# Attention's score maxima reach their contraction row by one transfer per head, and a query tile takes every fourth query

## The chip, the cores and the metric

The kernel runs on one core of one Trainium2 chip. The metric is device time in microseconds (us) of one execution; lower is better. Profiles come from one profiled execution of the same program. The engines are named as in the profile: PE is TensorE's matmul, PEld its weight load, DVE is VectorE, ACT is ScalarE, POOL is GpSimd, and SP is the queue that issues nearly all DMA transfers.

## The reference, cut to what matters

Eight sequences (`B = 8`) of 512 tokens with 512 features go through one decoder layer in float32: a Mamba block, cross attention with 16 heads of 32 features, and a mixture of 32 experts, each with its residual and a layer norm. The change touches attention's softmax alone:

```python
qm = _split_heads(q @ Wq.T + bq)
km = _split_heads(k @ Wk.T + bk)
vm = _split_heads(v @ Wv.T + bv)
scores = jnp.einsum('bnlh,bnph->bnlp', qm, km) / np.sqrt(HEAD_DIM)
scores = jnp.where(mask, scores, MASK_FILL)
attn = jax.nn.softmax(scores, axis=-1)
out = jnp.einsum('bnlp,bnph->bnlh', attn, vm)
```

## The kernel before

**Three parts.** `layers` holds Mamba, attention and the shared expert (in the profile from 0 to about 3790 us), `experts` the 32 routed experts (to about 5270 us), `finish` the last layer norm. The change lies in `layers`.

**Two streams of work in one loop.** The main loop goes over 16 chunks (8 sequences, 2 chunks of 256 tokens each) and in each over 32 steps of Mamba's scan. A step has three large DVE instructions: `steps_in` (L494), `scan` (L501) and `collect` (L510), some 4.7 us in all. For each step ACT makes the decays `l_da` (L480) from rows that a DMA has repeated over partitions (`rep`, L428), and PE sums products of the scan into `py` (`products`, L519 and L521). Products of a step read the tile `h` (six buffers), so a later `steps_in` waits for them. Beside it the loop works off a list of side work, `todo`: attention and the shared expert of the sequence before it. Each entry has a weight, and the loop takes entries so that weights spent keep pace with steps done. The last sequence has no scan beside it: its attention runs by itself, from about 3600 to 3710 us.

**Attention of one sequence** (`units`). Heads go in eight pairs. The tiles `qa` and `ka` of a pair hold for each of its two heads 64 rows: 32 rows of queries (or keys), and 32 more for terms that are added to the scores by the same matmul. One of those rows of `qa` is for the maximum of each query, and the row of `ka` against it holds a constant. For a pair:

- `spread(i)` fills `qa` and `ka` and clears the row of maxima.
- `maximum(i, lt)`, four times: PE makes the scores of 128 queries (stationary: a slice of `qa`) against 512 keys, for both heads (L813), and DVE takes the maximum over keys, of both heads at once (L815), into two columns of the tile `mx`.
- `negate(i)`: PE transposes `mx` into a PSUM tile `ps_m` (four transposes, L822), ACT multiplies by -1 into a tile `nm` (L826), and two DMAs write its two rows into the row of maxima of `qa` (L829).
- `weigh(i, kc)`, four times: PE makes the scores the other way round, keys by queries, now with the maximum subtracted by the contraction itself (L839), and ACT takes the exponential (L843).
- `gather(i, kc)`: PE multiplies by the values (L855), the sums of weights come along.

`maximum` runs six places ahead of `weigh`, and the list alternates: a `maximum`, a `weigh`, a `gather`. Entries are made by

```python
if late:
    add(0.4, negate, late.pop(), dry=True)
if m < pairs * SC:
    add(0.9, maximum, m // SC, m % SC)
```

**What decides the order on an engine.** The functions emit instructions in the order of the loop, and a part that a function returns (a DVE or ACT instruction that reads what PE made) is emitted a little later. The framework then lays out each engine's instructions, and each engine works through its own in order. The score tiles `ps_s` and `ps_t` share two PSUM buffers (pool `l_pss`), so that a score matmul of `maximum` waits until the DVE maximum of the tile two before it is done. `ps_m` is one of the many users of the two buffers "mm" (pool `l_psm`), `nm` one of those of the two buffers "row" (pool `l_p3`).

Of the kernel before, what the change touches and what calls it, by code (L numbers as in the profile page):

```python
# [8 lines left out]
F32 = mybir.dt.float32  # L9
# [3 lines left out]
ALU = mybir.AluOpType  # L13
AX = mybir.AxisListType
# [3 lines left out]
P = 128  # L18
B, S, D = 8, 512, 512
DC = D // P  # L20
# [16 lines left out]
HD = 32  # L37
SC = S // P
# [50 lines left out]
def layers(ctx, tc, a, x1d, filld, based, xbuf):  # L89
# [23 lines left out]
    nc = tc.nc  # L113
# [3 lines left out]
    cp = ctx.enter_context(tc.tile_pool(name="l_const", bufs=1))  # L117
# [3 lines left out]
    p2 = ctx.enter_context(tc.tile_pool(name="l_p2", bufs=2))  # L121
    p3 = ctx.enter_context(tc.tile_pool(name="l_p3", bufs=2))
    dp = ctx.enter_context(tc.tile_pool(name="l_dram", bufs=2, space=DRAM))
    psm = ctx.enter_context(tc.tile_pool(name="l_psm", bufs=2, space=PSUM))
# [4 lines left out]
    ident = cp.tile([P, P], F32, name="l_ident")  # L129
# [7 lines left out]
    def rows(w):  # L137
        return w.rearrange("(c p) f -> p c f", p=P)
# [61 lines left out]

    ones = cp.tile([P, P], F32, name="l_ones")
    nc.gpsimd.memset(ones, 1.0)
    fold = cp.tile([P, QP], F32, name="l_fold")
    for at, sign in ((0, 1), (NQ - 1, -1)):
        nc.gpsimd.affine_select(
# [57 lines left out]
    def later_constants():  # L263

        nc.sync.dma_start(
            aneg.rearrange("p c j g -> p (c j) g"),
            a["A_log"].rearrange("(b c) (s g) -> (c s) b g", c=QP, s=NQ),
        )
        for i in range(NPB):
            for r0 in (HD + 1, 2 * HD + HD + 1):  # L270
                nc.sync.dma_start(
                    kas[i][r0 : r0 + 1, :].rearrange("p (c t) -> p c t", c=DC),
                    ones[0:1, :].unsqueeze(1).to_broadcast([1, DC, P]),
                )
        nc.sync.dma_start(bq, a["bq"])
        nc.sync.dma_start(bk, a["bk"])
        nc.sync.dma_start(bv, a["bv"].rearrange("(c p) -> p c", p=P))
        nc.sync.dma_start(bo, a["bo"].partition_broadcast(P))
        nc.sync.dma_start(wg, rows(a["wg"]))
# [473 lines left out]
    def units(b):  # L753

        st = {}
# [49 lines left out]
        def maximum(i, lt):  # L805

            qa, ka = st[i]
            if lt == 0:
                st["mx", i] = p2.tile([P, SC, 2], F32, tag="mx", name="mx")
            ps = pss.tile([P, 2, S], F32, tag="sc", name="ps_s")  # L810
            for j in range(2):
                r = slice(j * 2 * HD, (j + 1) * 2 * HD)
                nc.tensor.matmul(ps[:, j, :], qa[r, lt * P : (lt + 1) * P], ka[r, :], start=True, stop=True)  # L813
            mx = st["mx", i]
            return lambda: nc.vector.tensor_reduce(mx[:, lt, :].unsqueeze(2), ps, AX.X, ALU.max) and None  # L815

        def negate(i):

            mx = st.pop(("mx", i))
            pm = psm.tile([P, S], F32, tag="mm", name="ps_m")  # L820
            for lt in range(SC):
                nc.tensor.transpose(pm[0:2, lt * P : (lt + 1) * P], mx[:, lt, :], ident)  # L822

            def put():
                nm = p3.tile([P, D], F32, tag="row", name="nm")
                nc.scalar.mul(nm[0:2, :], pm[0:2, :], -1.0)  # L826
                for j in range(2):
                    r0 = j * 2 * HD + HD + 1
                    nc.sync.dma_start(st[i][0][r0 : r0 + 1, :], nm[j : j + 1, :])  # L829

            return put

        def weigh(i, kc):

# [128 lines left out]
        def add(weight, fn, *args, dry=False):  # L963

            todo.append((weight, lambda: fn(*args), dry))
# [14 lines left out]
        late = []  # L980

        def max_at(m):

            if late:
                add(0.4, negate, late.pop(), dry=True)
            if m < pairs * SC:
                add(0.9, maximum, m // SC, m % SC)
                if m % SC == SC - 1:
                    late.append(m // SC)

        for m in range(ahead):
            max_at(m)
        add(0, load, "sw1")
        for n in range(pairs * SC + 4):
            i, k = n // SC, n % SC
            if k == 0 and i + 2 < pairs:
                add(0, spread, i + 2)
            max_at(n + ahead)
            if i < pairs:
                add(0.9, weigh, i, k)  # L1000
            if 0 < n <= pairs * SC:
                add(0.9, gather, (n - 1) // SC, (n - 1) % SC)

            if n > 3 and (n - 3) % (2 * SC) == 0:
                add(0, divide, (n - 3) // (2 * SC) - 1, dry=(n > pairs * SC))
# [61 lines left out]
    def work(k):  # L1067

        front = 6.9 if k in (2, 3) else 3.4 if 4 <= k < 8 or k in (12, 14, 17, 20, 23) else 1.0 if k in (11, 25) else 0.0
        return 1.2 + front  # L1070
# [6 lines left out]
    for q in range(CC // 2):  # L1077
        do(convolve, 0, q, f, first=(q == 0))
    dry()
    later_constants()  # L1080
    silu(*f["xs"].values())
    do(x_proj, f)
# [16 lines left out]
    for i, (b, t) in enumerate(chunks):  # L1099
        nf = {}  # L1100
        after = chunks[i + 1] if i + 1 < len(chunks) else None
        if t == 0:
            side, spent = units(b - 1) if b else sources(0), 0.0

            own = [work(k) for k in range(len(steps))] * 2
# [411 lines left out]
def program(tc, a, out):  # L1517
    nc = tc.nc
    with tc.tile_pool(name="dram", bufs=1, space=DRAM) as dram:
        x1d = dram.tile([N, D], F32, name="x1d")  # L1520
        filld = dram.tile([B, S], F32, name="filld")

        based = dram.tile([N + P, D], F32, name="based")
        xbuf = dram.tile([SLOTS, ROW], F32, name="xbuf")
        nc.scalar.preload_act_table_set(LN_EXP)

        with ExitStack() as ctx:
            layers(ctx, tc, a, x1d, filld, based, xbuf)
        with ExitStack() as ctx:
            experts(ctx, tc, a, xbuf, based)  # L1530
        with ExitStack() as ctx:
            finish(ctx, tc, based, out)
# [31 lines left out]
```

## Time and profile before

| what | value |
| --- | --- |
| median of three runs | 5403.67 us (5400.97 to 5409.85) |
| profiled execution, its own time | 5406.28 us |
| span of its instructions | 5404.6 us |
| mean granted TensorE clock | 0.935 |
| PE, DVE, ACT, POOL busy over the span | 86%, 78%, 48%, 11% |
| 500 to 3520 us (scan with attention beside it): PE, DVE, ACT busy of 3020 us | 2545, 2748, 1779 us |
| 3600 to 3710 us (attention of the last sequence alone): PE, DVE, ACT busy of 110 us | 107, 45, 47 us |
| 3790 to 5270 us (experts): PE, DVE busy of 1480 us | 1473, 867 us |
| the transposes L822: count, busy | 256, 46.3 us |
| the ACT instructions L826: count, busy | 64, 37.2 us |
| the DMAs L829: count, time of one on SP's queue | 128, 553 ns (median) |

Busy time is the sum of an engine's instructions in a stretch. PE's times hold the time for which a matmul sits in the array behind another, so they overlap. An answer to "who waited for whom" names the instruction that waited, then what ended its wait, then the total, the number of times and the longest.

### The profile page before, as it was taken

Reading aid. Unit: us, or ns where it says so; the run is one execution under the profiler, and the core shown is the slowest. Engines: PE = TensorE matmul, PEld = TensorE weight load, DVE = VectorE, ACT = ScalarE, POOL = GpSimd, SP = SyncE. Lnnn points to the kernel's source line nnn. Section 1 sums busy time; section 2 is a strip of 40 time slices with the busy share of each in tenths; the row PEclk is TensorE's granted clock in tenths of the full one; section 3 lists DMA queues with packets and bytes.
Section 4 is the critical chain, followed back from the end, with each engine's and each line's share of the span. In section 5 each row is a group of like instructions: output and inputs, shape, how many; then the busy total and the mean of one; then the engine's idle time right before and its main releaser. Section 6 shows DMA issues by size and latency. Waiting matters only on the chain. (4 is left out here: it accounts for less than half of the span.)

```text
span 5404.6 us, 53991 instructions
## 1 busy us (share of the span) xinstructions
PE 4672.4 (86%) x17320; PEld 2476.6 (46%) x17320; DVE 4235.9 (78%) x5369; ACT 2593.6 (48%) x5726; POOL 570.3 (11%) x426
## 2 busy tenths in 40 slices
PE   6768889788888988988888888789999999999994
PEld 3324234234333423433333342333677777777773
DVE  7999899989989989898998998943566555665554
ACT  5566565565656556566565655523222222222223
POOL 1000002002000200200200020011111111111111
PEclk8879989999999999999999999899999999999997
DMA  8875346345444634634544463342344444544544
GB/s 236 266 224 146 87 96 208 81 114 176 114 104 117 197 77 109 189 98 107 174 125 100 117 200 78 91 146 66 103 128 127 123 117 118 127 127 121 129 115 144
DMA packets 486427, 719.03 MB, mean 133 GB/s; under 512 B 117137, under 2 KB 200625, under 8 KB 484096
## 3 DMA queue, kind: packets, MB, share of 16 engines
q1 hardware_dynamic: 450128, 627.16, 41.1%
q0 software_dynamic: 33280, 76.90, 7.5%
q10 hardware_dynamic: 2736, 11.54, 0.5%
q8 instruction: 137, 2.24, 0.2%
q14 instruction: 146, 1.20, 0.1%
HBM read 391.24 MB, written 165.05 MB: 103 GB/s over the span
## 5 line engine op out<-in xcount | busy, mean ns | idle before, releaser
L480 ACT ACTIVATE l_da<-rep,l_aneg 128x256 f32<-128x256 f32 x2048 | 895.0, 501 | 941.8 <-DVE h L501 877.0
L501 DVE TENSOR_TENSOR_SCAN h<-l_da,h 128x1028 f32<-128x1028 f32 x512 | 1166.0, 2292 | 20.3 <-ACT l_da L480 17.7
L494 DVE TENSOR_TENSOR h<-rep,bc 128x1024 f32<-128x1024 f32 x512 | 614.7, 1218 | 103.1 <-PE py L521 84.6
L510 DVE TENSOR_TENSOR h<-h,bc 128x1024 f32<-128x1024 f32 x512 | 619.5, 1217 | 2.1
L521 PE MATMUL py<-h,l_fold 128*32 128x512 f32 x2048 | 368.3, 644 | 113.4 <-DVE h L510 96.5
L813 PE MATMUL ps_s<-l_ka,l_qa 64*128 64x512 f32 x1024 | 325.6, 707 | 137.8 <-DVE mx L815 137.6
L1314 PE MATMUL ps_h<-xT,w 128*128 128x320 f32 x1536 | 435.8, 433 | 0.0
L1394 POOL DMA_INDIRECT based<-y,xe x160 | 255.5, 1597 | 1309.9 <-ACT y L1417 630.0
L1335 DVE TENSOR_TENSOR hT<-ps_h,p 128x320 f32<-128x320 f32 x128 | 62.9, 492 | 378.5 <-PE ps_h L1314 378.5
L815 DVE TENSOR_REDUCE mx<-ps_s 128x2 f32<-128x1024 f32 x256 | 310.2, 1217 | 58.5 <-PE ps_s L813 58.3
L1314 PEld LDWEIGHTS ps_h<-xT,w 128*128 128x128 f32 x1536 | 292.5, 191 | 118.3 <-issue 0.4
L855 PE MATMUL po<-eT,l_va 128*64 128x512 f32 x1024 | 301.5, 670 | 47.6 <-ACT eT L843 43.1
L839 PE MATMUL ps_t<-l_qa,l_ka 64*128 64x512 f32 x1024 | 308.4, 674 | 23.8 <-ACT eT L843 23.1
L843 ACT ACTIVATE eT<-ps_t 128x1024 f32<-128x1024 f32 x256 | 259.0, 1015 | 128.8 <-PE ps_t L839 128.5
L688 POOL DMA_INDIRECT xbuf<-x2t,dest x128 | 217.2, 1697 | 860.4 <-DVE dest L679 760.8
L1314 PE MATMUL ps_h<-t,s 128*128 128x320 f32 x1024 | 286.1, 432 | 0.0
L343 PE MATMUL ps_z<-xnT,wm 128*128 128x256 f32 x1024 | 238.0, 388 | 30.0 <-DVE o L561 24.3
L750 PE MATMUL ps_p<-x2T,wa 128*128 128x512 f32 x512 | 241.5, 626 | 18.1 <-ACT hT L944 10.4
L552 PE MATMUL po<-wm,zs 128*128 128x512 f32 x512 | 244.7, 632 | 13.8 <-DVE z L957 11.9
L343 PE MATMUL ps_x<-xnT,wm 128*128 128x256 f32 x1024 | 246.5, 393 | 4.5 <-ACT xnT L332 2.5
L343 PEld LDWEIGHTS ps_z<-xnT,wm 128*128 128x128 f32 x1024 | 194.6, 193 | 93.0 <-DVE o L561 37.5
L343 PEld LDWEIGHTS ps_x<-xnT,wm 128*128 128x128 f32 x1024 | 196.1, 195 | 80.5 <-issue 43.8
(232 smaller groups left out, 7170.4 us busy)
## 6 DMA issues: line engine op xcount, KB each, us to landing
w<-in_w SPq DMA_DIRECT2D x93, 1024.0 KB
wm<-in_in_proj_w SPq DMA_DIRECT2D x128, 512.0 KB
rep<-dt SPq DMA_DIRECT2D x256, 256.0 KB
rep<-dtx SPq DMA_DIRECT2D x256, 256.0 KB
xbuf<-zero SPq DMA_DIRECT2D x32, 1362.5 KB
xe<-xbuf SPq DMA_DIRECT2D x32, 1362.5 KB
wm<-in_out_proj_w SPq DMA_DIRECT2D x64, 512.0 KB
wa<-in_sw SPq DMA_DIRECT2D x24, 1024.0 KB
```

Of the source, the lines that this page charges most:

```text
L343: nc.tensor.matmul(ps[:, i, :], w[:, dc, i * P : (i + 1) * P], f["xnT"][:, dc, :], start=(dc == 0), stop=(dc == DC - 1),)
L480: nc.scalar.activation(da[:, n, 1:], dt[:, j, i, :], AF.Exp, scale=aneg[:, 2 * q + i, 2 * jj + j, g : g + 1])
L494: nc.vector.tensor_tensor(h[:, :, 1:], dtx.rearrange("p j i t -> p (j i) t"), f["bc", g][0], ALU.mult)
L501: nc.vector.tensor_tensor_scan(flat, da.rearrange("p n t -> p (n t)"), flat, 0.0, ALU.mult, ALU.add)
L510: nc.vector.tensor_tensor(h[:, :, 0:T], h[:, :, 1:], f["bc", g][1], ALU.mult)
L521: nc.tensor.matmul(f["py"][j * QP : (j + 1) * QP, :, :], fold, hs[j // 2][:, 2 * (j % 2) : 2 * (j % 2) + 2, 0:T], start=False, stop=g == N ...
L813: nc.tensor.matmul(ps[:, j, :], qa[r, lt * P : (lt + 1) * P], ka[r, :], start=True, stop=True)
L815: return lambda: nc.vector.tensor_reduce(mx[:, lt, :].unsqueeze(2), ps, AX.X, ALU.max) and None
L839: nc.tensor.matmul(ps[:, j, :], ka[r, kc * P : (kc + 1) * P], qa[r, :], start=True, stop=True)
L843: nc.scalar.activation(eT, ps, AF.Exp)
L855: nc.tensor.matmul(po[j * 2 * HD : (j + 1) * 2 * HD, :], va[:, kc, i, j * HD : (j + 2) * HD], eT[:, j, :], start=(kc == 0), stop=(kc == SC ...
L1314: nc.tensor.matmul(ps, w[:, n, r * P : (r + 1) * P], x[:, n, :], start=not more and n == 0, stop=n == 1, skip_group_check=more,)
```

## The change

The constant row of `ka` becomes -1 (it was 1), so that the row of `qa` takes the maxima as they are. Nothing has to be negated. A query tile `lt` no longer holds queries 128 lt to 128 lt + 127, but the queries lt, lt + 4, lt + 8 and so on: every fourth. Partition p of `mx` then holds the maxima of queries 4p to 4p + 3, and with its axes exchanged (`[P, 2, SC]`) these four lie side by side for each head. Read partition by partition, a head's 128 by 4 maxima are its 512 queries in order, and one DMA per head carries them from `mx` straight into the row of `qa`. The transposes, the PSUM tile, the ACT instruction and the tile `nm` are gone. The entry's weight goes from 0.4 to 0.

```diff
+    minus = cp.tile([1, P], F32, name="l_minus")
+    nc.gpsimd.memset(minus, -1.0)
...
                 nc.sync.dma_start(
                     kas[i][r0 : r0 + 1, :].rearrange("p (c t) -> p c t", c=DC),
-                    ones[0:1, :].unsqueeze(1).to_broadcast([1, DC, P]),
+                    minus.unsqueeze(1).to_broadcast([1, DC, P]),
                 )
...
             if lt == 0:
-                st["mx", i] = p2.tile([P, SC, 2], F32, tag="mx", name="mx")
+                st["mx", i] = p2.tile([P, 2, SC], F32, tag="mx", name="mx")
             ps = pss.tile([P, 2, S], F32, tag="sc", name="ps_s")
             for j in range(2):
                 r = slice(j * 2 * HD, (j + 1) * 2 * HD)
-                nc.tensor.matmul(ps[:, j, :], qa[r, lt * P : (lt + 1) * P], ka[r, :], start=True, stop=True)
+                own = qa[r, :].rearrange("k (p l) -> k l p", l=SC)[:, lt, :]
+                nc.tensor.matmul(ps[:, j, :], own, ka[r, :], start=True, stop=True)
             mx = st["mx", i]
-            return lambda: nc.vector.tensor_reduce(mx[:, lt, :].unsqueeze(2), ps, AX.X, ALU.max) and None
-
-        def negate(i):
+            return lambda: nc.vector.tensor_reduce(mx[:, :, lt].unsqueeze(2), ps, AX.X, ALU.max) and None
+
+        def subtract(i):
 
             mx = st.pop(("mx", i))
-            pm = psm.tile([P, S], F32, tag="mm", name="ps_m")
-            for lt in range(SC):
-                nc.tensor.transpose(pm[0:2, lt * P : (lt + 1) * P], mx[:, lt, :], ident)
-
-            def put():
-                nm = p3.tile([P, D], F32, tag="row", name="nm")
-                nc.scalar.mul(nm[0:2, :], pm[0:2, :], -1.0)
-                for j in range(2):
-                    r0 = j * 2 * HD + HD + 1
-                    nc.sync.dma_start(st[i][0][r0 : r0 + 1, :], nm[j : j + 1, :])
-
-            return put
+            for j in range(2):
+                r0 = j * 2 * HD + HD + 1
+                nc.sync.dma_start(st[i][0][r0 : r0 + 1, :], mx[:, j, :])
...
             if late:
-                add(0.4, negate, late.pop(), dry=True)
+                add(0, subtract, late.pop(), dry=True)
```

## The prediction

> **What bounds the kernel now.** I read the page first: the busy shares and the 40 slices.
>
> ```profile
> PE 4672.4 (86%) x17320; PEld 2476.6 (46%) x17320; DVE 4235.9 (78%) x5369; ACT 2593.6 (48%) x5726; POOL 570.3 (11%) x426
> ...
> PE   6768889788888988988888888789999999999994
> DVE  7999899989989989898998998943566555665554
> ```
>
> DVE is full up to slice 26, where the scan runs with attention beside it. In slices 27 and 28 the last sequence's attention runs alone, and behind them PE is full with the experts, which the change doesn't touch. In the table by stages DVE is busy for 2748 of the 3020 us from 500 to 3520 us, so at most 272 us can be gained there, and only where DVE stands idle. From 3600 to 3710 us PE is busy for 107 of 110 us: there PE's work counts in full.
>
> The waits of DVE from 500 to 3520 us (who waited, for what: us, times, longest) say what its idle time is made of:
>
> ```profile
> DVE h L494 <- PE py L521: 84.6, 35, 5.4
> DVE m L73 <- ACT r L69: 33.5, 26, 3.3
> DVE dtx L457 <- ACT dtx L453: 28.5, 22, 3.1
> DVE xs L377 <- ACT xs L369: 27.0, 14, 4.1
> DVE h L501 <- ACT l_da L480: 17.7, 7, 2.8
> DVE mx L815 <- PE ps_s L813: 14.0, 17, 1.4
> ```
>
> No line names a maximum's way to its row. It can only cost through PE (`py` late) or ACT. PE's own waits in that stretch:
>
> ```profile
> PE ps_s L813 <- DVE mx L815: 137.1, 94, 4.2
> PE ps_m L822 <- DVE mx L815: 74.9, 35, 3.4
> ```
>
> The second looks like the prize: PE stands for 74.9 us before transposes that go away. The timeline of PE at the longest kind of these waits (start, us, what; in brackets the idle time before) tells otherwise:
>
> ```profile
> 1513.74 1.08 PE L855 MATMUL po<-eT,l_va 128*64 128x512 f32 x4
> 1514.75 0.49 PE L822 MATMUL ps_m<-l_ident,mx 128*2 128x128 f32 x3
> 1518.47 0.37 PE L822 MATMUL ps_m<-l_ident,mx 128*2 128x128 f32 x1 [3.23 <-DVE mx L815]
> 1518.77 2.18 PE L813 MATMUL ps_s<-l_ka,l_qa 64*128 64x512 f32 x4
> ...
> 1524.31 1.07 PE L521 MATMUL py<-h,l_fold 128*32 128x512 f32 x8
> ```
>
> The fourth transpose waits for the maximum that ends at 1518.41. But behind it stands a score product, and it needs the PSUM buffer which the same maximum reads (two buffers, used in turn by `ps_s` and `ps_t`). Without the transposes it waits there just as long. I counted over all 64 places: of the 74.9 us of waiting, 71.7 stand ahead of a score product and 3.2 ahead of `py`. The wait stays under another name; what goes is the transposes' own time.
>
> **What is removed.** Sums are made against the profiled execution (5406.3 us; span 5404.6, so 1.7 lie around it). The median of the runs is 2.6 us below it.
>
> Last sequence, 3600 to 3710 us. PE goes round a loop of three products, and a transpose group is inserted once per pair:
>
> ```profile
> 3638.10 1.08 PE L855 MATMUL po<-eT,l_va 128*64 128x512 f32 x4
> 3639.11 0.60 PE L822 MATMUL ps_m<-l_ident,mx 128*2 128x128 f32 x4
> 3639.64 1.13 PE L813 MATMUL ps_s<-l_ka,l_qa 64*128 64x512 f32 x4
> ```
>
> From 3639.11 to 3639.64 is 0.53 us; eight pairs make -4.2 us. At the first pair the way to the row is exposed: DMA 1.1 us after the maximum's end, first weight load of `weigh` 2.8 us after it. Without transpose and ACT the DMA starts about 1 us earlier; I take -0.8.
>
> 500 to 3520 us, 56 pairs. PE loses 41 us and ACT 33 us of work, nearly all beside a DVE that is busy. It counts where DVE waits behind it. Of the 84.6 us for `py`, 37 (7 times 5.3) stand behind the output projection (L552), which doesn't change. Of the rest, three waits per sequence (1.3, 2.6, 3.1 us) lie behind chains like that above, where transposes of 0.3 to 0.5 us stand in the chain: 7 x 3 x 0.4 = -8 us. Of the waits for `xs` (ACT) 24 us fall within 8 us of a transpose group; one `nm` of 0.58 us per sequence in front of it gives -4. Bounds: 0, and -64, which is all DVE idle time within 8 us behind a transpose group; chance alone would put a fifth of the idle time there, so I stay with the chains.
>
> **What is added.** The weight load of the score product now reads every fourth float. No row shows such a load. The contiguous row: a load of 128 columns takes 186 ns (L813, median), of 2 columns 82 ns (L822), so 0.83 ns a column. Where it can't hide it is seen in the matmul: 693 ns (L813, median) against 589 (its minimum), 104 ns. It is exposed once per score product, since the buffer's wait holds the load back; the second load hides behind a 0.43 us pass. Below, the cost is 0 (as contiguous). Above, four times the bytes passed over for each float used: +0.32 us per product. If the rate halves, +0.106 us: 32 products of the last sequence +3.4, and two products in each of the 21 chains +4.5, together +8. I take half of that, +4, since the nearest row is the contiguous one and nothing excludes the other.
>
> The Trainium skill speaks against this edit: "SBUF — State Buffer", section on door 1, says that lines of SBUF have 16 bytes and that full bandwidth needs at least two hits in a line, while in the same breath it calls a stride of four floats free. No run here shows which holds. By the first reading, taken as half the rate, the sum below would be 4 us higher, by the second 4 us lower.
>
> The transfers. Each row now comes as 128 pieces of 16 bytes instead of 16 of 128. On SP the nearest rows are `bc` (L418, 128 pieces): 573 ns, and `va` (L765, 1024 pieces): 617 ns, against 553 for L829. That is +0.02 to +0.06 us for each of 128, at most 8 us on a queue whose time hides under DVE: 0 on the path. In the trace's packets 16 bytes take 9 ns and 128 bytes 13, so the 16 DMA engines hardly notice. Landing: in the interleaved pairs behind the first, the first load of `weigh` comes 7 us or more after the last maximum, and the transfer starts 1 to 3 us earlier than now. If that cover were gone, a microsecond later would cost a microsecond per pair, 56 at most.
>
> SP's queue. The transfer now waits for DVE's maximum, no longer for ACT's `nm` (124 us in 22 waits). In the built order it passes ahead of three `bc` transfers in the third pair of a sequence and of one or two `rep` in the fourth, sixth and seventh. These are queued behind the waiting transfer, and ACT's decays wait for `rep` (46.9 us in 31 waits). But the maximum is done 1 to 7 us before the transfers start today, so SP is freed earlier. Bounds -8 and +4; I take 0. The DVE instruction that writes `mx` in another order, the constant row and the shorter rotation of "mm" and "row" buffers cost nothing that a row shows.
>
> The order. Removing an entry's weight and its instructions shifts others: in DVE's built order instructions move by a few places. One `py` wait of 3.1 us more or less in each of seven sequences is +-22 us. It has no sign; I keep it for the range.
>
> Sum: -4.2 - 0.8 - 8 - 4 + 4 = -13 us: 5406.3 - 13 = 5393.3 in the profiled execution, 5390.7 in the median of the runs.
>
> **The rivals.**
>
> *Hidden anyway.* DVE's chain takes none of the interleaved savings: -5 in the last sequence, +4 for the loads: about 5403. For it: DVE is 91% busy and no line names the chain. Against it: PE runs without a pause from 1518.47 into the DVE wait.
>
> *Slower: `py` behind a score product.* In the built order two `py` groups per sequence that followed a transpose group, or stood together, are now behind one more score product (one is even split, three of its four products coming later). A score product takes 0.96 us, and it waits for a maximum, 1.5 us on average (137.1 / 94). Where DVE then finds its `h` buffer taken this costs up to 2.5 us: 14 x 2.5 = +35, less the 17 saved: 5404 + 18 = 5422. It decides from about half of that, where DVE has no other work ahead of L494. Against it: the transposes held `py` back as well.
>
> *Slower: the load at a quarter of the rate.* +0.32 x 32 + 0.32 x 42 = +24, less 17: 5411, and up to 5430 if DVE's maxima (14.0 us of waits now) come later too. It decides from about 0.25 us per load.
>
> *More.* SP and the buffers freed early take away half of the 64 us: 5370.
>
> **How the numbers follow.** From no change at all a measurement here tells about 0.2%, 11 us. Forecast (11 to 30 us faster) 0.38; more than that 0.10; hidden anyway 0.20; `py` later 0.20; slow loads 0.12. So faster 0.48, same 0.20, slower 0.32. The range leaves out the far half of the "more" case and the tail of the slower ones: 5365 to 5425. The forecast's own range is 5374 to 5393.
>
> **What would show it.** Right: L813's waits for `mx` grow to about 209 us as L822 vanishes; DVE's wait for `py` falls by some 8 us; the loop of the last sequence runs 2.93 us a turn without the 0.53 us inserts; the DMAs stay under 0.62 us on SP. Wrong: a PEld median of L813 well over 186 ns and matmuls over 693 ns (slow loads); a `py` wait that grows (order); PE of the last sequence waiting for `qa`<-`mx` (the transfer itself). I would be most surprised if L813's wait stayed at 137 us and the time fell by over 40.

## The result and the profile after

The changed kernel is slower: 5445.56 us in the median of 8 runs (5431.0 to 5468.89), against 5403.88 for the kernel before (8 runs). The ratio is 1.0080, with a 95% interval from 1.0064 to 1.0096. The profiled execution took 5444.95 us, its span 5443.0. The forecast was 5391, with a range to 5425: wrong in sign, and outside the range.

Lines behind L202 are two to three higher than before at first, and four to six lower behind the function that changed: L494, L501, L510 and L521 are now L496, L503, L512 and L523; the chain L457 to L460 is L459 to L462; L813 and L815 are L816 and L818; the transfer L829 is L825.

First the page, in the same two places as before: the busy shares, and the slices of PE and DVE.

```profile
PE 4698.4 (86%) x17064; PEld 2525.3 (46%) x17064; DVE 4233.6 (78%) x5369; ACT 2581.7 (47%) x5669; POOL 488.1 (9%) x427
...
PE   6768888888888888888888888789899999999994
DVE  7999898988988989898898998953465556665554
```

The 256 transposes and the 64 ACT instructions that negated are gone, DVE's work is the same to 2.3 us, and PEld is 49 us busier although it has 256 loads fewer. DVE's row holds more eights than before up to slice 26. So DVE does the same work with more idle time in it. Its waits from 500 to 3560 us (who waited, for what: total, times, longest) say for what; they answer to the DVE waits that the prediction shows of before:

```profile
DVE h L496 <- PE py L523: 115.0, 56, 5.3
DVE dtx L459 <- ACT dtx L455: 50.7, 13, 4.9
DVE h L496 <- DMA rep<-dtx: 40.8, 12, 5.4
...
DVE xs L379 <- ACT xs L371: 10.5, 7, 2.1
```

`py` costs 30.4 us more (84.6 before), the wait for ACT's part of the `dtx` chain 22.2 more (28.5 before), and the third line is new among the large ones: DVE waits 40.8 us for the repeated rows that a DMA makes from `dtx`. The waits for `xs` fell by 16.5. Before, the line of the repeated rows, and PE's wait for `h` that is read next, were:

```profile
DVE h L494 <- DMA rep<-dtx: 6.5, 6, 1.6
...
PE py L521 <- DVE h L510: 15.4, 14, 4.7
```

PE's waits in the same stretch of the changed kernel:

```profile
PE ps_s L816 <- DVE mx L818: 199.2, 101, 3.5
PE py L523 <- DVE h L512: 61.5, 7, 9.7
```

The first is the wait that the forecast said would only change its name (137.1 + 74.9 before). The second was 15.4 us in 14 waits; now it is 61.5 us in 7, up to 9.7 us each.

Last, the score product's weight load and matmul (ns: least, median, most), before and then after:

```profile
L813 PEld LDWEIGHTS ps_s<-l_ka,l_qa x1024: 182/186/335, 502.5 to 3685.3; 64*128 64x128 f32 x171
L813 PE MATMUL ps_s<-l_ka,l_qa x1024: 589/693/1220, 502.5 to 3685.7; 64*128 64x512 f32 x171
```

```profile
L816 PEld LDWEIGHTS ps_s<-l_ka,l_qa x1024: 304/306/334, 514.4 to 3722.3; 64*128 64x128 f32 x171
L816 PE MATMUL ps_s<-l_ka,l_qa x1024: 589/815/1240, 514.4 to 3722.8; 64*128 64x512 f32 x171
```

Both medians rise by 120 ns or a little more. The attention of the last sequence, from the first pair's last maximum to the last product with the values, takes 96.1 us against 96.7, and the experts are as before. So the loss (38 us between the two profiled executions, 42 between the medians) lies where the scan runs.

From the traces I worked out one more number for every kernel below: DVE's idle time between the first scan of the second sequence and the last scan of all, counting gaps of over 0.1 us. DVE's busy time there is 2853 to 2862 us in every kernel; the idle time differs by far more, 263.7 us before and 307.4 after.

### The profile page after: what moved, and what is told of

It reads as the page before. It is cut to its first block, busy times and chain, and to the rows that moved or that the text cites. A ratio compares the mean times of both kernels' runs of the same rounds, so it can differ in the third digit from the quotient of the medians.

```text
span 5443.0 us, 53398 instructions
## 1 busy us (share of the span) xinstructions
PE 4698.4 (86%) x17064; PEld 2525.3 (46%) x17064; DVE 4233.6 (78%) x5369; ACT 2581.7 (47%) x5669; POOL 488.1 (9%) x427
## 5 line engine op out<-in xcount | busy, mean ns | idle before, releaser
L503 DVE TENSOR_TENSOR_SCAN h<-l_da,h 128x1028 f32<-128x1028 f32 x512 | 1165.3, 2291 | 15.3 <-ACT l_da L482 14.1
L496 DVE TENSOR_TENSOR h<-rep,bc 128x1024 f32<-128x1024 f32 x512 | 613.0, 1217 | 174.2 <-PE py L523 115.0
L512 DVE TENSOR_TENSOR h<-h,bc 128x1024 f32<-128x1024 f32 x512 | 618.9, 1218 | 1.5
L523 PE MATMUL py<-h,l_fold 128*32 128x512 f32 x2048 | 402.4, 663 | 155.7 <-DVE h L512 140.2
L816 PE MATMUL ps_s<-l_ka,l_qa 64*128 64x512 f32 x1024 | 346.0, 752 | 200.9 <-DVE mx L818 200.7
L818 DVE TENSOR_REDUCE mx<-ps_s 128x2 f32<-128x1024 f32 x256 | 310.2, 1217 | 63.7 <-PE ps_s L816 63.5
L816 PEld LDWEIGHTS ps_s<-l_ka,l_qa 64*128 64x128 f32 x1024 | 144.1, 316 | 407.9 <-DVE mx L818 317.6
L345 PEld LDWEIGHTS ps_z<-xnT,wm 128*128 128x128 f32 x1024 | 198.5, 197 | 94.1 <-DVE o L563 36.9
L523 PEld LDWEIGHTS py<-h,l_fold 128*32 128x32 f32 x2048 | 56.9, 112 | 391.5 <-DVE h L512 165.3
```

The source lines that it names most:

```text
L345: nc.tensor.matmul(ps[:, i, :], w[:, dc, i * P : (i + 1) * P], f["xnT"][:, dc, :], start=(dc == 0), stop=(dc == DC - 1),)
L496: nc.vector.tensor_tensor(h[:, :, 1:], dtx.rearrange("p j i t -> p (j i) t"), f["bc", g][0], ALU.mult)
L503: nc.vector.tensor_tensor_scan(flat, da.rearrange("p n t -> p (n t)"), flat, 0.0, ALU.mult, ALU.add)
L512: nc.vector.tensor_tensor(h[:, :, 0:T], h[:, :, 1:], f["bc", g][1], ALU.mult)
L523: nc.tensor.matmul(f["py"][j * QP : (j + 1) * QP, :, :], fold, hs[j // 2][:, 2 * (j % 2) : 2 * (j % 2) + 2, 0:T], start=False, stop=g == N ...
L816: nc.tensor.matmul(ps[:, j, :], own, ka[r, :], start=True, stop=True)
```

## The experiments

Three theories were there at the start. ORDER: the entry's weight, which goes from 0.4 to 0, moves other entries of the list, and that order costs the time. LOAD: the strided weight load costs it. TRANSFER: the row's new way costs it. Ratios are against the kernel before, run beside each on the same chip.

**Three parts by themselves.** The kernel before with strided tiles alone:

```diff
-                nc.tensor.matmul(ps[:, j, :], qa[r, lt * P : (lt + 1) * P], ka[r, :], start=True, stop=True)
+                own = qa[r, :].rearrange("k (p l) -> k l p", l=SC)[:, lt, :]
+                nc.tensor.matmul(ps[:, j, :], own, ka[r, :], start=True, stop=True)
```

> The kernel before with one edit: the score product's stationary tile takes every fourth query, as in the change; transposes, ACT's negation and weight 0.4 stay, and every engine's instructions stand in the order of before. (The maxima so land on other queries of the same head; what is subtracted is only permuted.) The changed kernel's profile has the load at 306 ns against 186. Theory LOAD (the slower weight load is the loss): nearly all of the 42 us and of the 17 us that were to be saved show here, 5440 us or more. Theory ORDER (the entry's weight of 0 rearranged the whole stretch and that is the loss): 0.12 us times 32 products of the last sequence (+4) and 42 in chains ahead of a waiting DVE (+5), 5409 to 5415 us.

Measured: 5412.19 us, ratio 1.0014 (1.0005 to 1.0023). The kernel before with the weight alone changed:

```diff
-                add(0.4, negate, late.pop(), dry=True)
+                add(0, negate, late.pop(), dry=True)
```

> The kernel before with one edit: the entry of negate in the list of side work has weight 0, no longer 0.4. The same instructions, in another order. ORDER: 5430 to 5455 us, with the waits that the changed kernel has: DVE's L494 for rep<-dtx some 40 us (6.5 before) and PE's py for h some 60 us. LOAD: 5398 to 5410 us, no change.

Measured: 5438.17 us, ratio 1.0060 (1.0046 to 1.0074). One number in a list costs 0.6%, with the same instructions as the kernel before in another order. And its DVE waits (500 to 3560 us) have the new line of the changed kernel:

```profile
DVE h L494 <- PE py L521: 113.5, 54, 5.4
DVE dtx L457 <- ACT dtx L453: 50.4, 13, 4.9
DVE h L494 <- DMA rep<-dtx: 42.2, 10, 4.7
```

These are the changed kernel's 115.0, 50.7 and 40.8 within 1.5 us. Now the changed kernel with the weight of before:

```diff
-                add(0, subtract, late.pop(), dry=True)
+                add(0.4, subtract, late.pop(), dry=True)
```

> The changed kernel with one edit: the entry of subtract has weight 0.4 as negate had. Its instructions then stand almost in the order of before. ORDER: the loss is gone: 5390 to 5403 us (17 us saved, 4 to 9 lost to the slower load). LOAD: 5440 us or more, as the change.

Measured: 5395.91 us, ratio 0.9982 (0.9974 to 0.9991). With the order kept, the change is faster than the kernel before. Then the same with contiguous tiles:

> The changed kernel with weight 0.4 and with contiguous query tiles, so no slow weight load (the maxima land on other queries of the same head). What is left of the change is the transfer in place of transposes and ACT. Both theories: 5384 to 5392 us, the 17 us of the prediction. A third theory, TRANSFER (128 pieces of 16 bytes arrive late or hold up SP): above 5404 us.

Measured: 5390.16 us, ratio 0.9975 (0.9964 to 0.9985). So the transfer in place of transposes and ACT saves 0.25%, or 13.5 us. TRANSFER has fallen. ORDER is shown as a cause; that it is not the only one comes out below.

**Which of the moved entries?** In each sequence weight 0 places 23 entries elsewhere than 0.4 does, nearly all of them one step away: four ahead of attention a step later, and of attention's own and those behind it five later and fourteen earlier. Adding a small weight at one entry and taking it off at another moves only what lies between. Ahead of attention alone (on weight 0.4):

```diff
-        add(0, begin)
+        add(0.6, begin)
...
-        add(0, spread, 0)
+        add(-0.6, spread, 0)
```

> The version with weight 0.4 for the transfer's entry (5395.91 us), and in it only the entries ahead of attention (values, keys, queries of the sequence: two of them, and a flip) pushed a step later, as weight 0 pushes them; attention and what is behind it stay at their steps. HEAD (what stands ahead of attention makes the loss): 5435 to 5445. ATT or TAIL (attention's own entries, or those behind it): 5393 to 5400. SPREAD (every move costs a little, by the number of entries moved, 3 of 23): about 5402.

Measured: 5393.73 us, ratio 0.9971 (0.9962 to 0.9981). Nothing lost. Two entries behind attention alone (-0.65 at the `fetch` behind attention, +0.65 at the first `shared`):

> The version with weight 0.4 (5395.91 us), and in it only entries behind attention (the output projection and the shared expert: two of them) taken a step earlier, as weight 0 takes them. TAIL: 5430 to 5445, with DVE's 4.6 us waits for the repeated rows at the start of a sequence's steps back (12 in all). HEAD or ATT: 5393 to 5400. SPREAD: about 5400.

Measured: 5407.51 us, ratio 1.0005 (0.9995 to 1.0015). That is 12 us more than weight 0.4's order; the profiled execution, the second shortest of 12, took 5396.54 us and has no more `rep` waits than weight 0.4's (8.1 us against 9.4), so its trace can't say where the 12 us are. The reverse of the first, weight 0 with the entries ahead of attention put back (-0.5 and +0.5):

> The changed kernel, weight 0 (5445.56 us), and in it the entries ahead of attention put back to their steps of before; attention and what is behind it stay moved. HEAD: 5396 to 5405. ATT or TAIL: 5438 to 5450. SPREAD: about 5437.

Measured: 5441.14 us, ratio 1.0068 (1.0052 to 1.0084). HEAD has fallen twice. Attention's first pairs alone (on 0.4; +0.5 at the first `spread`, -0.5 at the fifth):

> The version with weight 0.4 (5395.91 us), with four entries of attention's first pairs placed a step later, as weight 0 places them, and two more that come with it. FIRST HALF: 5425 to 5445. LATE HALF: 5393 to 5400. SUM: 5400 to 5410.

Measured: 5388.49 us, ratio 0.9972 (0.9962 to 0.9982). Attention's late half alone (-0.9 at the seventh `spread`, +0.9 at the `fetch` behind attention):

> The version with weight 0.4 (5395.91 us), with attention's entries from pair 5's last maximum on placed as weight 0 places them (eleven entries a step earlier, and one more); everything ahead of them and behind attention stays. LATE HALF (these make most of the 50 us between 5395.91 and the changed kernel's 5445.56): 5425 to 5445, and the waits of 5 us for rep behind dtx come back (40 us in all). FIRST HALF: 5393 to 5402. SUM (no part by itself): 5402 to 5415.

Measured: 5399.24 us, ratio 0.9991 (0.9979 to 1.0003). Four entries of that half (-0.5 and +0.5 in the same places):

> The version with weight 0.4, with four of the eleven late entries alone placed as weight 0 places them: pair 5's last maximum, one maximum and one gather of pairs 7 and 5, and pair 7's transfer, all a step earlier. If the first of them, a maximum that moves over the border of a chunk, brings the waits for rep: 5420 to 5440. If not, and the others of the eleven do: 5393 to 5402.

Measured: 5414.79 us, ratio 1.0026 (1.0016 to 1.0036). All three expectations of a culprit in attention missed. Four entries of a group cost 19 us against 0.4's order by the medians (0.44% by the ratios), the whole group 3 (0.09%, inside the intervals). Moves don't add up. In the trace of the four, DVE's wait for `py` is well above the 100.3 us of weight 0.4's order, and `rep` is where it was (9.2 against 9.4):

```profile
DVE h L496 <- PE py L523: 122.9, 53, 6.4
```

So an order can also cost by `py` alone.

**The strided load in weight 0's order.** The changed kernel with contiguous tiles:

```diff
-                own = qa[r, :].rearrange("k (p l) -> k l p", l=SC)[:, lt, :]
+                own = qa[r, lt * P : (lt + 1) * P]
```

> The changed kernel with weight 0 as it is, with the query tiles contiguous again, so that maxima land on other queries than their own; its instructions stand exactly in the changed kernel's order. LOAD (the 306 ns weight load costs 6 to 10 us, as it did with weight 0.4): 5436 to 5440. If in this order the load costs nothing, since DVE's waits cover it: 5443 to 5448. If the slow load is what the order turns on: 5400 to 5415.

Measured: 5416.42 us, ratio 1.0027 (1.0017 to 1.0037), with DVE idle for 282.2 us. In this order the load costs 29 us, not 4 to 6: none of the three expectations had it, though the third, 5400 to 5415, ends just below it. The order of the instructions is the changed kernel's, so it is the load's price and no new order. So two causes were there, and the entry was still not found.

**One entry.** Until here groups were moved. The traces show another difference: where DVE's chain of four instructions (L459 to L462), from which the next chunk's `dtx` and its repeated rows come, stands among the scans. In four kernels (the changed one, the one before with weight 0, and at weight 0 the one with entries put back ahead of attention and the one with contiguous tiles) it stands behind the last scan of a sequence in six sequences; in all others measured so far it stands ahead of the last two scans. (The expectations count finished scans and say "behind step 0" for behind the last one of a chunk.) In the built programs one moved entry was found that brings this about: the second product of the output projection, which was in none of the groups moved by themselves. It goes one step earlier alone, on weight 0.4:

```diff
-        add(0, fetch, 0)
+        add(-0.75, fetch, 0)
...
-            add(3.4, output, lt, dry=(lt == 0))
+            add(3.4 + (0.75 if lt == 1 else 0), output, lt, dry=(lt == 0))
```

> The version with weight 0.4 (5395.91 us), and in it one entry alone placed as weight 0 places it: the second product of the output projection goes from step 17 of a sequence's second chunk to step 16. In the built order of DVE this moves the four-instruction chain that prepares dtx for the next sequence from step 30 to behind step 0 of the next chunk, in six sequences, as in the four kernels measured at weight 0 and in none of the others. CHAIN (this is what weight 0 costs): 5425 to 5445, the waits of 5 us for rep behind dtx and of 9.7 us for h back. LOTTERY (no single place decides, the order as a whole does): 5390 to 5415.

Measured: 5428.24 us, ratio 1.0047 (1.0035 to 1.0060). One entry by one step costs 32 us. Two DVE waits of 500 to 3560 us, with weight 0.4 and then with the one entry moved:

```profile
DVE h L496 <- PE py L523: 100.3, 47, 7.0
...
DVE h L496 <- DMA rep<-dtx: 9.4, 7, 2.3
```

```profile
DVE h L496 <- PE py L523: 116.5, 52, 6.9
...
DVE h L496 <- DMA rep<-dtx: 25.8, 17, 3.1
```

The time and the `rep` waits go the way that CHAIN expects, but the waits are up to 3.1 us, not 5, PE's waits for `h` last up to 4.7 us, not 9.7, and `py` rises by as much as `rep`. DVE's timeline at the end of a sequence (start, us, what; in brackets the idle time before), with weight 0.4 and then with the one entry moved:

```profile
1724.00 0.69 DVE L459 SCALAR_TENSOR_TENSOR dtx<-dtx,u 128x512 f32<-128x512 f32 x1 [0.58 <-ACT dtx L455]
...
1727.51 0.69 DVE L462 TENSOR_TENSOR dtx<-dt,xs 128x512 f32<-128x512 f32 x1
...
1731.61 2.29 DVE L503 TENSOR_TENSOR_SCAN h<-l_da,h 128x1028 f32<-128x1028 f32 x1
...
1735.93 2.29 DVE L503 TENSOR_TENSOR_SCAN h<-l_da,h 128x1028 f32<-128x1028 f32 x1
...
1740.51 2.35 DVE L496 TENSOR_TENSOR h<-rep,bc 128x1024 f32<-128x1024 f32 x2
```

```profile
1732.33 2.29 DVE L503 TENSOR_TENSOR_SCAN h<-l_da,h 128x1028 f32<-128x1028 f32 x1
...
1737.66 0.66 DVE L459 SCALAR_TENSOR_TENSOR dtx<-dtx,u 128x512 f32<-128x512 f32 x1
...
1740.04 0.68 DVE L462 TENSOR_TENSOR dtx<-dt,xs 128x512 f32<-128x512 f32 x1
...
1748.06 1.23 DVE L496 TENSOR_TENSOR h<-rep,bc 128x1024 f32<-128x1024 f32 x1 [2.17 <-DMA rep<-dtx]
...
1756.56 1.23 DVE L496 TENSOR_TENSOR h<-rep,bc 128x1024 f32<-128x1024 f32 x1 [1.61 <-DMA rep<-dtx]
```

In the first, two scans stand between the chain's end (1728.2) and the new chunk's first large instruction (1740.51): 12.3 us in which the DMA repeats the rows. In the second the chain ends at 1740.72, behind the last scan. DVE starts the new chunk 7.3 us behind the chain's end, has waited 2.17 us for rows by then, and waits 1.61 us more for the next ones. The reverse, weight 0 with that entry alone put back (+0.3 at `fetch`, -0.3 at the second `output`):

> The changed kernel with weight 0 (5445.56 us), and in it that one entry put back from step 16 to step 17, nothing else. The chain returns to steps 30 and 31. CHAIN: 5395 to 5412, with rep's wait gone. LOTTERY: 5430 to 5450.

Measured: 5403.39 us, ratio 1.0001 (0.9990 to 1.0013): 42 us below the changed kernel. Its DVE waits, against the changed kernel's:

```profile
DVE h L496 <- PE py L523: 103.2, 58, 5.3
DVE dtx L459 <- ACT dtx L455: 50.6, 13, 4.9
...
DVE h L496 <- DMA rep<-dtx: 11.5, 11, 1.3
```

The `rep` wait is nearly gone (40.8 to 11.5), and PE's 61.5 us for `h` L512 are 15.6; the chain stands ahead of the last scan again. Of the 46.3 us by which DVE's idle time falls, `rep` makes 29.3 and `py` 11.8. The wait for ACT's `dtx`, 50.6, stays: it belongs to weight 0's other moves and does not decide.

That the one entry costs this is shown both ways. That it costs it by the late chain is read from the waits: the chain was not moved by itself, and with the entry the layout puts other DVE instructions behind another number of scans too (630 of the 4857 that are not scans, from weight 0.4 to the one entry moved).

**What the load costs where.** The one-entry run with contiguous tiles, and the one put back with contiguous tiles:

> As the run that moves the one entry, with contiguous query tiles, so that maxima land on other queries than their own. If the strided weight load costs more where the chain is late (28 us at weight 0 against 6 at weight 0.4): 20 to 30 us below that run. If the 28 us belong to weight 0's order and not to the late chain: 3 to 10 us below it.

Measured: 5422.83 us, ratio 1.0038 (1.0025 to 1.0051), 5 us below the strided run: the late chain alone does not make the load dear.

> As the run that puts the one entry back at weight 0 (5403.39 us), with contiguous query tiles, so that maxima land on other queries than their own. If the strided load's price of 29 us at weight 0 needs the late chain as well as weight 0's other moves: 5395 to 5400 here. If weight 0's other moves alone make it dear: 5372 to 5382.

Measured: 5372.33 us, ratio 0.9943 (0.9930 to 0.9957), 31 us below the strided run: with weight 0's other moves it is dear without the late chain too. Its `py` wait is 92.9 us from 500 to 3500, against 103.2 with strided tiles in the same order, and its DVE idle time 237.8 against 261.1.

**Another way to the row.** Eight transfers per pair, with contiguous tiles (on weight 0.4):

```diff
-                nc.sync.dma_start(st[i][0][r0 : r0 + 1, :], mx[:, j, :])
+                for lt in range(SC):
+                    nc.sync.dma_start(st[i][0][r0 : r0 + 1, lt * P : (lt + 1) * P], mx[:, j, lt : lt + 1])
```

> Weight 0.4, query tiles contiguous again, and the row filled by eight transfers per pair (one per head and query tile, 128 pieces of 4 bytes each) instead of two of 128 pieces of 16 bytes, so that the output is the reference's without a strided weight load. LOAD: the weight load is back at 186 ns, and the time at the 5390 us of the version that only left the stride out. QUEUE: six more transfers a pair at 0.55 us are 3.3 us of SP's queue, 26 us per sequence, ahead of the repeated rows: SP sets the pace at places, DVE waits for rep, 5400 to 5440.

Measured: 5409.29 us, ratio 1.0008 (0.9999 to 1.0017). The load is back at 186 ns and one transfer of 4-byte pieces takes 551 ns, but DVE now waits 36.4 us for `rep` behind `dtx` (6.2 with two transfers): QUEUE holds, by repeated rows that are late for another reason. At DVE's wait of 4.08 us before 1527.32, for one, SP issues the repeated row at 1523.62 us, right behind three of the row's transfers (1521.75 to 1523.57).

**A better place.** The changed kernel at weight 0.1, and the kernel before at weight 0.1:

> The changed kernel with weight 0.1: eleven entries stand at weight 0's steps, the second output product stays at step 17 and the chain at step 30. CHAIN: 5390 to 5410. LOTTERY: anything from 5390 to 5445, the nearer to weight 0's the more it shares with it.

Measured: 5366.53 us (5360.3 to 5368.05), ratio 0.9933 (0.9920 to 0.9946). This beats both kernels; DVE's idle time is 229.9 us.

> The kernel before, with its transposes, its ACT instruction and its contiguous tiles, and the weight of the entry at 0.1 in place of 0.4. If the 5366.53 us of the changed kernel at weight 0.1 come from the order that this weight makes: 5365 to 5385, with the change itself worth 0 to 10 us in it. If they come from the change in that order: 5395 to 5410.

Measured: 5397.50 us, ratio 0.9989 (0.9980 to 0.9998). The weight alone gives 0.1%; the rest comes with the change. The two programs differ in PE's order by more than the transposes, so these 31 us can't be put down to one mechanism. DVE's waits of the best version (500 to 3560 us):

```profile
DVE h L496 <- PE py L523: 61.3, 40, 3.2
DVE dtx L459 <- ACT dtx L455: 54.7, 21, 4.9
```

The ratios by placement; the intervals are 0.0008 to 0.0016 to either side:

| placement of the list | transposes, contiguous | transfer, contiguous | transfer, strided |
| --- | --- | --- | --- |
| weight 0.4 | 1 | 0.9975 | 0.9982 |
| weight 0.4, one entry moved | not run | 1.0038 | 1.0047 |
| weight 0, that entry put back | not run | 0.9943 | 1.0001 |
| weight 0 | 1.0060 | 1.0027 | 1.0080 |
| weight 0.1 | 0.9989 | not run | 0.9933 |

Read down the last two columns: the one entry costs 0.63% and 0.65% at weight 0.4, 0.84% and 0.79% at weight 0. Read across: the stride costs 0.07% and 0.09% at weight 0.4, which is no more than the intervals, and 0.58% and 0.53% at weight 0. In the kernel before, not in the table, it costs 0.14%. Weight 0's other moves, without the one entry, save 0.32% with contiguous tiles (0.9975 to 0.9943) and cost 0.19% with strided ones.

## Why the prediction was wrong

**The step that failed** is the paragraph on the order: "One `py` wait of 3.1 us more or less in each of seven sequences is +-22 us. It has no sign; I keep it for the range." The order had a sign and a larger price: with the contiguous load it costs 0.52% (0.9975 to 1.0027), 28 us. The place of the chain could have been read from the built program; its price is known from the runs alone. I priced it by a `py` wait, the largest line of the profile, and looked in the built order only for `py`, the transfer and SP's queue. I did not look for a chain that feeds the next chunk. The dtx chain stood two scans later in six sequences, and behind it hang a DMA, and behind that the first large instructions of DVE.

**The load's term, +4 us,** had a good unit price and a bad count. The half-rate estimate was +0.106 us a load; measured are +0.120. I counted it in the 32 products of the last sequence and in 42 behind waiting chains, 74 of 256, and then took half of it. All 256 at 0.12 us are 31 us, and as much is what weight 0's order pays (29 and 31 us); 0.4's order pays 4 or 5, the kernel before about 8. Why the one order pays the price of nearly every load and the other that of a sixth was not traced to single waits. The count was made on the trace of before and so in the order of before; it does not carry over to an order that the same change makes.

**What is removed** was about right. The sum without the load was -17 us; the version with contiguous tiles and weight 0.4 is 13.5 us faster. The last sequence's share was smaller than forecast: its attention takes 94.1 us there against 96.7, a saving of 2.6 for -5.0. In the changed kernel a turn of its loop takes 3.05 us, the forecast 2.93 plus the load's 0.12.

**PE's wait** passed to the score product as forecast: 226.2 us at weight 0.4 and 236.1 with contiguous tiles, for "about 209" and for the 212.0 of the two lines before.

**The transfers** cost nothing, as forecast: 547 ns on SP against 553, and in the changed kernel no engine's wait names the row's transfer. The Trainium skill, "DMA: Bandwidth & Descriptors", section "Why small descriptors are slow (HBM only)", says that transfers within SBUF don't suffer the penalty of small descriptors. The time of the issue on SP agrees down to 4-byte pieces (551 ns). The pieces themselves are not free: in the trace's packets 4 or 16 bytes take 9 ns and 128 bytes 13, so a row takes 1.15 us of packet time in 128 pieces and 0.21 in 16, spread over the DMA engines; no wait shows it.

**The rivals.** Two signs that the prediction named for being wrong came: a weight load well over 186 ns (306) and a `py` wait that grows (84.6 to 115.0). "`py` behind a score product" had the sign and, at 5422, less than half of the loss, and `py` waits did grow by 30.4 us. But putting one entry back took 42 us off while `py` only fell from 115.0 to 103.2, so its mechanism is not what decides there. It is not nothing either: moving that entry on weight 0.4 raised `py` by 16.2 us beside 16.4 for `rep`. "The load at a quarter of the rate" had the wrong rate and, at 5411, a part of the loss. Each was priced by itself; the result has both causes at once.

**What stays open.** Why the layout moves the chain by two scans when one product goes a step earlier was not traced, nor was the chain moved without the entry. Nor was it shown why four moved entries make `py` wait 22.6 us longer and cost 19 us, and the group they belong to 3.

## What to carry to other kernels

A weight or a priority of a scheduler is a part of a change like any other: change it in a run of its own, or keep it and take only the instructions out. Before a forecast, compare where each producer chain of the next stage stands in the two built orders, above all chains that end in a DMA, and not only the instructions that the change touches. And a price per instruction times a count made in the old order is a bound, not a forecast: the full count belongs in the range.

## What the hardware showed

A weight load of 128 float32 columns takes 306 ns when it reads every fourth float and 186 ns when they are side by side, +0.94 ns a column. Where it can't hide, the matmul's median grows by 122 ns. The Trainium skill, "TensorE: Matmul & The Clock Gate", section "LDWEIGHTS (loading the stationary operand)", lets the time depend on the number of columns alone; these runs show that the stride counts too, at the same 128 columns. Of the two readings of "SBUF — State Buffer", section on door 1, that the prediction weighed, the one with a penalty holds for this operand, and the one that calls a stride of four floats free does not.
